# Head norm in a fused attention block: squares and last multiplication on GpSimd, inverse roots spread by DMA

## The chip, the cores and the metric

The kernel runs on one core of a Trainium2 chip. Times are microseconds of device time of one launch; less is better. The core's engines work side by side, each through its own queue in order, and hand work to each other by semaphores: TensorE (PE; PEld is its weight load), VectorE (DVE), ScalarE (ACT), GpSimd (POOL), and SyncE (SP), which here issues DMAs. Matrix products land in PSUM, eight banks of 128 x 512 numbers in float32; everything else is in SBUF.

## The reference

Input x has shape 8 x 512 x 512 (batch, token, feature), all in float32. Three residual steps follow each other: half of an expert layer on the normalised x (softmax router over 16 experts, the 256 best tokens of each expert, one expert matrix), a differential attention on the normalised x, and the same expert layer again. Attention, cut to what matters here:

```
q = rope(x @ Wq)   # 16 heads, each of two halves of D = 32
k = rope(x @ Wk)   # 4 key heads, each used by 4 heads
scores = softmax(causal(q . k / sqrt(D)))            # of both halves
diff = softmax(causal(scores[:, 0] - lam * scores[:, 1]))
att = diff @ v
att = att * rsqrt(mean(att * att over D) + 1e-8) * rms_w   # the head norm
att = att * (1 - LAM_INIT)
out = att.reshape(b, s, E) @ Wo
```

The head norm is what the change touches. It has one factor for each token and head: the inverse root of the mean of 32 squares.

## The kernel before, in words

The expert layers and a short preparation stand at the two ends; attention fills the time between some 220 and 1300 us. It is one loop written out by hand: `for k in range(K + 13)`, K = 176 passes, 22 for each of the 8 batches. A batch has two phases of 11 passes, one for each pair of key heads (`gp` 0 and 1); a pass is one "block", a part of a tile of 128 tokens. In pass k the engines work on several blocks at once, each at another stage: scores of block k + 1 (`scores`, L761), energies and first exponentials of block k (L777 on VectorE, L790 on ScalarE), `mask`, `factors` and `weigh` of block k - 1 on GpSimd (L828, L804, L814), then its `difference` on VectorE (L848), second exponentials of block k - 2 (`exps2`, L862), transposes of an earlier block (L882, copied by L898 and L900), and values (L913, copied by L926). `difference` reads what `weigh` writes.

Work that is not tied to a block is put into named slots of a pass by `at(offset, slot, fn)`, and `fill(k, slot)` emits it there. The slots in the order of a pass are "short" (after the transposes and values), "act mid" and "mid" (after the exponentials), "long" and "long 2" (large products; the next scores stand before, between or behind them, by the list PLACES), "dve" (before `difference`), "act" (the end of ScalarE's pass) and "pool" (the end of GpSimd's; its first instruction is made to wait for the pass's last difference). `rope_steps` projects q and k for the next phase (L635), multiplies by cosine and sine on VectorE (L654, L656), swaps neighbouring rows by two DMAs on SP's queue (L662) and adds on GpSimd (L665). `norm_steps` normalises the next batch's x (h, L574, turned at L582).

`finish_steps` is the head norm and the output projection of one tile of 128 tokens, 32 tiles in all. Its parts stand at offsets o0 to o4 of a phase. The four offsets of a tile in the first phase after its batch, or in the second phase of it, are in `plan`; the last two tiles of the last batch take theirs from LAST.

- `square` (o0, "act"): ScalarE squares the 128 x 512 attention values aT (L683). The values are not divided by z, the sum of the second softmax, so the term 1e-8 becomes 1e-8 z squared: two more squares of z, scaled by the root of 1e-8, for even and odd heads (L685, the tile u).
- `sums` (o1, "short"): TensorE sums the squares of each head with the matrix hsum (L694) into 4 of 32 rows of ss, and adds u by products with the matrix both (L700).
- `root` (o1, "act mid"): ScalarE takes the logarithm and the exponential of -0.5 of it, which is the inverse root r (L707, L708). Rows without a head get a constant idle, so that the logarithm has an argument.
- `turn` (o3, "short"): sixteen small TensorE products with a row of the identity copy each row of r to the 32 rows of its head (L715), into a PSUM bank.
- `norm` (o3, "dve"): VectorE multiplies aT by that (L723).
- `pe` (o4, "long" and "long 2") and `residual` (one pass later, "mid"): the output projection (L731) and the addition to x (L737).

PSUM banks 6 and 7 (MISC) go in turn to the values, the projections, ss, the spread factors and the output projection: each takes the bank that was taken two before, and waits for its reader.

Of the kernel before, what the change touches and what calls it, by code (L numbers as in the profile page):

```python
# [16 lines left out]
P = 128  # L17
# [5 lines left out]
R = H // KVH  # L23
Q = P // 2
NEXP = 16
TOPK = B * S // NEXP
# [15 lines left out]
def macaron_kernel(  # L42
# [46 lines left out]
    for base, mult in ((0, 1), (D - 1, -1)):  # L89
        nc.gpsimd.affine_select(  # L90
            out=hsum, in_=hsum, compare_op=ALU.is_ge, fill=0.0, base=base,
            pattern=[[-D * mult, 32]], channel_multiplier=mult,
        )

    idle = keep.tile([P, 1], F32, name="idle")
    nc.vector.tensor_reduce(
        idle, ident.rearrange("p (c k) -> p c k", c=4)[:, :, 4:], AX.XY, ALU.add
    )

# [55 lines left out]

    LAST = ((0, 1, 1, 2, 3), (3, 4, 4, 5, 6))

# [385 lines left out]
    def attention(f0, f1, home, first_end, projections_end, drain):  # L543
# [128 lines left out]
        def finish_steps(at, os, b, i, st):  # L672

            name = f"f{b}_{i}"
            t = {}

            def square():
                t["sq"] = home["sq"].tile([P, 4, P], F32, name=f"{name}_sq", tag="sq", bufs=2)

                t["u"] = tiny.tile([P, 2, 4, 4], F32, name=f"{name}_u", tag="u")  # L680
                z2 = st["z2"][:, i * H : (i + 1) * H]
                uh = t["u"].rearrange("p f c (q h) -> p (f c q) h", h=2)
                nc.scalar.activation(t["sq"], st["aT"][i], AF.Square)  # L683
                for h in range(2):
                    nc.scalar.activation(  # L685
                        uh[:, :, h], z2, AF.Square, scale=root_eps[:, h : h + 1]
                    )

            def sums():


                t["ss"] = misc(f"{name}_ss")
                for c in range(4):
                    nc.tensor.matmul(  # L694
                        t["ss"][32 * c : 32 * (c + 1), :P], hsum, t["sq"][:, c, :],
                        start=True, stop=False, tile_position=(0, 32 * c),
                    )
                for f in range(2):
                    for c in range(4):
                        nc.tensor.matmul(  # L700
                            t["ss"][32 * c : 32 * c + 4, f * Q : (f + 1) * Q], t["u"][:, f, c],
                            both, start=False, stop=(f == 1), tile_position=(0, 32 * c),
                        )

            def root():
                r = t["r"] = tiny.tile([P, P], F32, name=f"{name}_r", tag="r")
# [3 lines left out]
            def turn():  # L710

                t["f"] = misc(f"{name}_f")
                for c in range(4):
                    for q in range(4):
                        nc.tensor.matmul(  # L715
                            t["f"][q * D : (q + 1) * D, c * P : (c + 1) * P],
                            ident[:, 32 * c + q : 32 * c + q + 1].to_broadcast([P, D]), t["r"],
                            start=True, stop=True, tile_position=(0, q * D),
                        )

            def norm():
                t["an"] = home["sq"].tile([P, 4, P], F32, name=f"{name}_an", tag="sq", bufs=2)
# [15 lines left out]

            o0, o1, o2, o3, o4 = os
# [6 lines left out]
            at(o4, "long 2", lambda: pe(1))  # L746
            at(o4 + 1, "mid", residual)

# [237 lines left out]
        def plan(ph):  # L986
# [3 lines left out]
            if gp == 0:  # L990
# [77 lines left out]
        for k in range(K + 13):  # L1068
# [274 lines left out]
```

## Time and profile before

| what | value |
|---|---|
| median of 3 runs (lowest to highest) | 1422.42 us (1417.44 to 1423.59) |
| span of the profiled execution | 1420.2 us |
| TensorE's granted clock over the span | 0.969 |
| ScalarE: square of aT, L683 | 32 x 632 ns |
| ScalarE: squares of z, L685 | 64 x 302 ns |
| TensorE: spreading products, L715 | 35.0 us in 32 tiles |
| VectorE: last multiplication, L723 | 32 x 683 ns |
| GpSimd: rope addition of 128 x 512, L665 | 80 x 1296 ns |
| SP: swap by DMA, L662 | 160, 128 KB each, 2.0 us to landing |

The profile is of one execution; its own time is its span. A row of a group gives line, engine, operation, what is written and read, the count, then busy us and mean ns of one, then the engine's idle time just before and who ended it. A row of a time line gives start, length, then the same. The chain is the work that ended last, followed back from the end of the launch: what stands on it set the time.

### The profile page before, as it was taken

Reading aid. Unit: us, or ns where it says so; the run is one execution under the profiler, and the core shown is the slowest. Engines: PE = TensorE matmul, PEld = TensorE weight load, DVE = VectorE, ACT = ScalarE, POOL = GpSimd, SP = SyncE. Lnnn points to the kernel's source line nnn. Section 1 sums busy time; section 2 is a strip of 40 time slices with the busy share of each in tenths; the row PEclk is TensorE's granted clock in tenths of the full one; section 3 lists DMA queues with packets and bytes.
Section 4 is the critical chain, followed back from the end, with each engine's and each line's share of the span. In section 5 each row is a group of like instructions: output and inputs, shape, how many; then the busy total and the mean of one; then the engine's idle time right before and its main releaser. Section 6 shows DMA issues by size and latency. Waiting matters only on the chain.

```text
span 1420.2 us, 30675 instructions
## 1 busy us (share of the span) xinstructions
PE 1328.5 (94%) x9774; PEld 738.4 (52%) x9774; DVE 1154.9 (81%) x4405; ACT 1047.0 (74%) x3644; POOL 685.4 (48%) x1314
## 2 busy tenths in 40 slices
PE   6999899899999999999999999999999997998998
PEld 4544444455555555555555555555455555555443
DVE  6554769899989988998999899889989989654566
ACT  3411128999899898989898998989899989844110
POOL 5433626554555455454545555554545555443230
PEclk9999988999999999999999999999999997999999
DMA  9300011000000101000000001010000001000006
GB/s 344 91 1 0 0 38 38 9 31 24 16 24 17 39 1 38 9 31 9 32 24 16 28 13 39 2 38 16 24 13 27 28 13 40 1 5 1 1 1 236
DMA packets 27554, 48.19 MB, mean 34 GB/s; under 512 B 4720, under 2 KB 6016, under 8 KB 27392
## 3 DMA queue, kind: packets, MB, share of 16 engines
q1 hardware_dynamic: 25152, 42.03, 8.3%
q10 hardware_dynamic: 2208, 4.19, 0.8%
q8 instruction: 77, 1.26, 0.4%
q14 instruction: 85, 0.70, 0.2%
q0 software_dynamic: 32, 0.01, 0.0%
HBM read 16.86 MB, written 8.39 MB: 18 GB/s over the span
## 4 chain that ended last, share of the span: by engine, by line
PE 60%; ACT 13%; DVE 10%; issue 2%; POOL 0%; ACTq 0%; DVEq 0%
PE r_ps L635 18%; PE sc L761 8%; PE f_o L731 8%; ACT e L790 7%; PE tp L882 6%; PE yps L381 6%; PE av L913 4%; DVE e L777 4%; DVE t L848 3%; ACT t L862 2%; PE vps L610 2%; PE kps L403 2%; PE f_f L715 1%; ACT eT L900 1%; PE tp L325 1%
## 5 line engine op out<-in xcount | busy, mean ns | idle before, releaser
L790 ACT ACTIVATE e<-e,nb 128x192 f32<-128x192 f32 (+7 forms) x1024 | 535.5, 532 | 6.5 <-DVE nb L777 4.3
L777 DVE CUSTOM_DVE_ANT_0 e<-sc,mpos 128x192 f32<-128x192 f32 (+7 forms) x1024 | 400.8, 453 | 23.7 <-PE sc L761 16.5
L814 POOL TENSOR_SCALAR e<-e,z 128x512 f32<-128x512 f32 (+7 forms) x512 | 295.9, 590 | 16.7
L862 ACT ACTIVATE t<-t,nm 128x512 f32<-128x512 f32 (+7 forms) x512 | 270.0, 534 | 42.2 <-DVE nm L848 42.0
L761 PE MATMUL sc<-r,r 32*128 32x64 f32 (+7 forms) x2048 | 245.3, 456 | 10.8 <-DVE nb L777 4.9
L848 DVE CUSTOM_DVE_ANT_0 t<-e,z 128x512 f32<-128x512 f32 (+7 forms) x512 | 240.6, 518 | 5.1 <-POOL e L814 4.2
L635 PE MATMUL r_ps<-hT,wq_sb 128*128 128x512 f32 x512 | 235.6, 601 | 0.1
L381 PE MATMUL yps<-we,y 128*128 128x512 f32 x456 | 216.5, 612 | 1.0 <-ACT y L388 0.7
L882 PEld LDWEIGHTS tp<-ident,t 128*128 128x128 f32 x1280 | 146.5, 144 | 135.6 <-ACT eT L900 43.3
L882 PE MATMUL tp<-ident,t 128*128 128x128 f32 x1280 | 188.6, 283 | 28.1 <-ACT eT L900 26.6
L790 ACT ACTIVATION_READ_ACCUMULATOR e<-e,nb 128x1 f32 x1024 | 202.1, 197 | 0.0
L665 POOL TENSOR_TENSOR r<-r,r_sw 128x512 f32<-128x512 f32 x80 | 103.0, 1296 | 175.8 <-DVE z L799 84.2
L761 PEld LDWEIGHTS sc<-r,r 32*128 32x128 f32 x2048 | 117.4, 188 | 90.7 <-DVE nb L777 44.6
L391 POOL TENSOR_TENSOR y<-y,eb 128x512 f32<-128x512 f32 x57 | 73.1, 1283 | 164.4 <-ACT y L388 134.3
L635 PEld LDWEIGHTS r_ps<-hT,wq_sb 128*128 128x128 f32 x512 | 93.0, 190 | 113.9 <-issue 99.6
L388 ACT COPY y<-yps 128x512 f32<-128x512 f32 x57 | 33.4, 586 | 155.6 <-PE yps L381 155.6
L828 POOL TENSOR_SCALAR_AFFINE_SELECT e<-e 128x128 f32<-128x128 f32 x256 | 79.2, 316 | 99.4 <-ACT e L790 99.4
L898 DVE COPY eT<-tp 128x512 f32<-128x512 f32 (+1 forms) x176 | 112.0, 636 | 16.6 <-PE tp L882 16.6
L381 PEld LDWEIGHTS yps<-we,y 128*128 128x128 f32 x456 | 81.3, 192 | 78.4 <-issue 73.6
L731 PE MATMUL f_o<-wo_sb,f_an 128*128 128x512 f32 x256 | 118.6, 605 | 0.0
L804 POOL TENSOR_TENSOR z<-z,over 128x4 f32<-128x4 f32 (+1 forms) x192 | 38.0, 201 | 142.6 <-DVE z L799 142.5
L862 ACT ACTIVATION_READ_ACCUMULATOR t<-t,nm 128x1 f32 x512 | 100.4, 196 | 0.0
(123 smaller groups left out, 1668.6 us busy)
## 6 DMA issues: line engine op xcount, KB each, us to landing
r_sw<-r_by SPq DMA_DIRECT2D x160, 128.0 KB, 2.0
x<-in_x_dram SPq DMA_DIRECT2D x6, 1024.0 KB, 13.2
out_dram<-x SPq DMA_DIRECT2D x6, 512.0 KB, 3.2
out_dram<-x ACTq DMA_DIRECT2D x6, 512.0 KB, 3.2
x<-in_x_dram SPq DMA_DIRECT2D x8, 256.0 KB, 8.2
we<-in_expert_w_dram SPq DMA_DIRECT2D x2, 1024.0 KB, 7.7
wq_sb<-in_wq_dram SPq DMA_DIRECT2D x1, 2048.0 KB, 13.9
wo_sb<-in_wo_dram SPq DMA_DIRECT2D x8, 128.0 KB, 2.8
```

The source lines that it names most:

```text
L381: nc.tensor.matmul(held["yps"], buf[b][:, i, c * P : (c + 1) * P], held["we"][:, c, :], start=(c == 0), stop=(c == EC - 1),)
L635: nc.tensor.matmul(t["ps"], w[:, c, c0 : c0 + P], st["hT"][:, c, :], start=(c == 0), stop=(c == EC - 1),)
L665: return nc.gpsimd.tensor_add(t["out"], t["out"], t["sw"])
L731: nc.tensor.matmul(t["o"], t["an"][:, c, :], wo_sb[:, c // 2, c % 2, :], start=(c == 0), stop=(c == 3),)
L761: nc.tensor.matmul(u["sc"][j][:, part.cols], q[j * D : (j + 1) * D, q0 : q0 + P], kq["k"][j * D : (j + 1) * D, : part.n], start=True, stop ...
L777: nc.vector.tensor_tensor_reduce(out=u["e"][:, j, part.cols], in0=u["sc"][j][:, part.cols], in1=mpos[:, S - part.n :], scale=1.0, scalar=3 ...
L790: nc.scalar.activation(e, e, AF.Exp, bias=u["nb"][:, c : c + 1], scale=-1.0, accum_out=u["z"][:, 0, c : c + 1],)
L814: nc.gpsimd.tensor_scalar(e, e, u["z"][:, 1, c : c + 1], u["z"][:, 0, c - nr : c - nr + 1], ALU.mult, ALU.mult,)
L848: u["diff"] = nc.vector.tensor_tensor_reduce(out=u["t"][:, par, r * w : r * w + part.n], in0=u["e"][:, 2 * par, s], in1=u["e"][:, 2 * par ...
L862: nc.scalar.activation(t, t, AF.Exp, bias=u["nm"][:, par, r : r + 1], scale=-1.0, accum_out=z2[:, col : col + 1],)
L882: nc.tensor.transpose(u["tp"][par][:, o : o + P], u["t"][:, par, (r * (i + 1) + c) * P : (r * (i + 1) + c + 1) * P], ident,)
L898: nc.vector.tensor_copy(o, s)
```

## The change

Squares and last multiplication move to GpSimd for 30 tiles; the last two tiles of the last batch keep the old way, under the names `square_late`, `turn_late` and `norm_late`. The matrix hsum and the tile u are made eightfold (REP = 8), so that all 32 rows of a group of four heads hold a sum, each head in eight equal rows; u is written by GpSimd from z squared and a constant, two instructions of 128 x 128 a tile. The root no longer needs the constant idle. The sums move from the slot "short" to a new slot "sums" ahead of "long", the root from "act mid" to "act". The spreading products are replaced by four DMAs on SP's queue (`spread`), each reading 32 rows of r and writing every row to four rows, into the tile that held the squares; the last multiplication is done there in place. h no longer shares buffers with the squares.

```diff
@@ hsum, constants
-            pattern=[[-D * mult, 32]], channel_multiplier=mult,
+            pattern=[[-D * mult, 4], [0, REP]], channel_multiplier=mult,
...
+    eps_of = keep.tile([P, 2], F32, name="eps_of")
+    nc.vector.tensor_scalar(eps_of, parity, RMS_EPS, None, ALU.mult)
...
-    LAST = ((0, 1, 1, 2, 3), (3, 4, 4, 5, 6))
+    LAST = ((0, 1, 2, 3), (3, 4, 5, 6))
@@ finish_steps
+            def factor_tile():
+                t["u"] = tiny.tile([P, 2, 4, 4 * REP], F32, name=f"{name}_u", tag="u", bufs=1)
+                return t["u"].rearrange("p f c (q h w) -> p (f c q) h w", h=2, w=REP)
+
             def square():
                 t["sq"] = home["sq"].tile([P, 4, P], F32, name=f"{name}_sq", tag="sq", bufs=2)
-                nc.scalar.activation(t["sq"], st["aT"][i], AF.Square)
-                for h in range(2):
-                    nc.scalar.activation(
-                        uh[:, :, h], z2, AF.Square, scale=root_eps[:, h : h + 1]
-                    )
+                first = nc.gpsimd.tensor_tensor(t["sq"], st["aT"][i], st["aT"][i], ALU.mult)
+                z2 = st["z2"][:, i * H : (i + 1) * H]
+                zz = tiny.tile([P, H], F32, name=f"{name}_zz", tag="zz", bufs=1)
+                nc.gpsimd.tensor_tensor(zz, z2, z2, ALU.mult)
+                uh = factor_tile()
+                for h in range(2):
+                    nc.gpsimd.tensor_scalar(
+                        uh[:, :, h], zz.unsqueeze(2).to_broadcast([P, H, REP]),
+                        eps_of[:, h : h + 1], None, ALU.mult,
+                    )
+                return first
...
-                            t["ss"][32 * c : 32 * c + 4, f * Q : (f + 1) * Q], t["u"][:, f, c],
-                            both, start=False, stop=(f == 1), tile_position=(0, 32 * c),
+                            t["ss"][32 * c : 32 * (c + 1), f * Q : (f + 1) * Q],
+                            t["u"][:, f, c], both, start=False, stop=(f == 1), tile_position=(0, 32 * c),
...
-                nc.scalar.activation(r, t["ss"][:, :P], AF.Ln, bias=idle)
+                nc.scalar.activation(r, t["ss"][:, :P], AF.Ln)
...
+            def spread():
+                for c in range(4):
+                    nc.sync.dma_start(
+                        t["sq"][:, c, :],
+                        t["r"][32 * c : 32 * (c + 1), :].unsqueeze(1).to_broadcast([32, D // REP, P]),
+                    )
+
+            def norm():
+                t["an"] = t["sq"]
+                return nc.gpsimd.tensor_tensor(t["an"], t["an"], st["aT"][i], ALU.mult)
...
-            at(o0, "act", square)
-            at(o1, "short", sums)
-            at(o1, "act mid", root)
-            at(o3, "short", turn)
-            at(o3, "dve", norm)
-            at(o4, "long", lambda: pe(0))
+            if b == B - 1 and i > 1:
+                at(o0, "act", square_late)
+                at(o1, "short", sums)
+                at(o1, "act mid", root)
+                at(o2, "short", turn_late)
+                at(o2, "dve", norm_late)
+            else:
+                at(o0, "pool", square)
+                at(o1, "sums", sums)
+                at(o1, "act", root)
+                at(o1, "act", spread)
+                at(o2, "pool", norm)
+            at(o3, "long", lambda: pe(0))
...
@@ plan
-                    finish_steps(at, (0, 1, 2, 4, 5) if b < B else LAST[0], b - 1, 2, sts[b - 1])
-                    finish_steps(at, (3, 5, 5, 7, 8) if b < B else LAST[1], b - 1, 3, sts[b - 1])
+                    finish_steps(at, (0, 1, 4, 5) if b < B else LAST[0], b - 1, 2, sts[b - 1])
+                    finish_steps(at, (3, 4, 7, 8) if b < B else LAST[1], b - 1, 3, sts[b - 1])
...
-                finish_steps(at, (4, 5, 5, 7, 9), b, 0, sts[b])
-                finish_steps(at, (6, 7, 7, 9, 10), b, 1, sts[b])
+                finish_steps(at, (4, 5, 7, 9), b, 0, sts[b])
+                finish_steps(at, (6, 7, 9, 10), b, 1, sts[b])
@@ the pass
+            fill(k, "sums")
             fill(k, "long")
@@ first_end
-        home.update(aT=opened["out"], sq=opened["out"], h=(opened["out"], "sq"))
+        home.update(aT=opened["out"], sq=opened["out"], h=(opened["out"], "h"))
```

More of the change, by code (lines that the diff above doesn't have):

```diff
@@ L24 @@
 Q = P // 2
+REP = 8
 NEXP = 16
@@ L90, in macaron_kernel @@
         nc.gpsimd.affine_select(
-            out=hsum, in_=hsum, compare_op=ALU.is_ge, fill=0.0, base=base,
-            pattern=[[-D * mult, 32]], channel_multiplier=mult,
-        )
-    idle = keep.tile([P, 1], F32, name="idle")
-    nc.vector.tensor_reduce(
-        idle, ident.rearrange("p (c k) -> p c k", c=4)[:, :, 4:], AX.XY, ALU.add
-    )
+            out=hsum.rearrange("p (q w) -> p q w", w=REP), in_=hsum.rearrange("p (q w) -> p q w", w=REP),
+            compare_op=ALU.is_ge, fill=0.0, base=base,
+            pattern=[[-D * mult, 4], [0, REP]], channel_multiplier=mult,
+        )
     parity = keep.tile([P, 2], F32, name="parity")
@@ L675, in finish_steps, with square_late @@
             t = {}
+            def factor_tile():
+                t["u"] = tiny.tile([P, 2, 4, 4 * REP], F32, name=f"{name}_u", tag="u", bufs=1)
+                return t["u"].rearrange("p f c (q h w) -> p (f c q) h w", h=2, w=REP)
             def square():
                 t["sq"] = home["sq"].tile([P, 4, P], F32, name=f"{name}_sq", tag="sq", bufs=2)
-                t["u"] = tiny.tile([P, 2, 4, 4], F32, name=f"{name}_u", tag="u")
+                first = nc.gpsimd.tensor_tensor(t["sq"], st["aT"][i], st["aT"][i], ALU.mult)
                 z2 = st["z2"][:, i * H : (i + 1) * H]
-                uh = t["u"].rearrange("p f c (q h) -> p (f c q) h", h=2)
+                zz = tiny.tile([P, H], F32, name=f"{name}_zz", tag="zz", bufs=1)
[7 more added lines that the diff above has]
+                return first
+            def square_late():
+                t["sq"] = home["sq"].tile([P, 4, P], F32, name=f"{name}_sq", tag="sq", bufs=2)
+                z2 = st["z2"][:, i * H : (i + 1) * H]
+                uh = factor_tile()
                 nc.scalar.activation(t["sq"], st["aT"][i], AF.Square)
@@ L685, in square @@
                     nc.scalar.activation(
-                        uh[:, :, h], z2, AF.Square, scale=root_eps[:, h : h + 1]
+                        uh[:, :, h], z2.unsqueeze(2).to_broadcast([P, H, REP]), AF.Square,
+                        scale=root_eps[:, h : h + 1],
                     )
@@ L700, in sums, with turn_late @@
                         nc.tensor.matmul(
-                            t["ss"][32 * c : 32 * c + 4, f * Q : (f + 1) * Q], t["u"][:, f, c],
-                            both, start=False, stop=(f == 1), tile_position=(0, 32 * c),
+                            t["ss"][32 * c : 32 * (c + 1), f * Q : (f + 1) * Q],
+                            t["u"][:, f, c], both, start=False, stop=(f == 1), tile_position=(0, 32 * c),
                         )
             def root():
-                r = t["r"] = tiny.tile([P, P], F32, name=f"{name}_r", tag="r")
-                nc.scalar.activation(r, t["ss"][:, :P], AF.Ln, bias=idle)
+                r = t["r"] = tiny.tile([P, P], F32, name=f"{name}_r", tag="r", bufs=1)
+                nc.scalar.activation(r, t["ss"][:, :P], AF.Ln)
                 nc.scalar.activation(r, r, AF.Exp, scale=-0.5)
-            def turn():
+            def spread():
[7 more added lines that the diff above has]
+                return nc.gpsimd.tensor_tensor(t["an"], t["an"], st["aT"][i], ALU.mult)
+            def turn_late():
                 t["f"] = misc(f"{name}_f")
@@ L716, in turn, with norm_late @@
                             t["f"][q * D : (q + 1) * D, c * P : (c + 1) * P],
-                            ident[:, 32 * c + q : 32 * c + q + 1].to_broadcast([P, D]), t["r"],
+                            ident[:, 32 * c + REP * q : 32 * c + REP * q + 1].to_broadcast([P, D]), t["r"],
                             start=True, stop=True, tile_position=(0, q * D),
                         )
-            def norm():
+            def norm_late():
                 t["an"] = home["sq"].tile([P, 4, P], F32, name=f"{name}_an", tag="sq", bufs=2)
@@ L737, in residual @@
                 nc.vector.tensor_add(x_sb[b][:, i, :], x_sb[b][:, i, :], t["o"])
-            o0, o1, o2, o3, o4 = os
-            at(o0, "act", square)
-            at(o1, "short", sums)
-            at(o1, "act mid", root)
-            at(o3, "short", turn)
-            at(o3, "dve", norm)
-            at(o4, "long", lambda: pe(0))
-            at(o4, "long 2", lambda: pe(1))
-            at(o4 + 1, "mid", residual)
+            o0, o1, o2, o3 = os
+            if b == B - 1 and i > 1:
[11 more added lines that the diff above has]
+            at(o3, "long", lambda: pe(0))
+            at(o3, "long 2", lambda: pe(1))
+            at(o3 + 1, "mid", residual)
         def scores(u):
```

## The prediction

> **What bounds the kernel now.** I read the page first (engine shares, the chain), then the table of stretches for one whole batch of attention, the chain in order of time over that batch, and last the time lines of GpSimd (POOL) and VectorE (DVE) in the passes where the change puts work. Page, parts 1 and 4:
>
> ```profile
> PE 1328.5 (94%) x9774; PEld 738.4 (52%) x9774; DVE 1154.9 (81%) x4405; ACT 1047.0 (74%) x3644; POOL 685.4 (48%) x1314
> ...
> PE 60%; ACT 13%; DVE 10%; issue 2%; POOL 0%; ACTq 0%; DVEq 0%
> ```
>
> One stretch of 135 us inside attention (start:end, length, then busy us of PE, PEld, DVE, ACT, POOL; the batch period is about 130 us):
>
> ```profile
> 740.00:875.00 135.00, 128.65 (x1127) 72.80 (x1126) 122.81 (x498) 125.22 (x456) 72.37 (x152) 0.99 0.06 23
> ```
>
> PE 95%, ACT 93%, DVE 91%: three engines are close to full at once, POOL is at 54%. So the kernel is not bound by one engine but by the order in which the three hand work to each other. The chain shows who leads where (start, length, what):
>
> ```profile
> 752.54 0.61 DVE r_by L656
> ...
> 753.19 1.08 PE f_f L715 x32
> ...
> 758.81 3.63 PE f_o L731 x8
> ...
> 828.67 0.53 ACT f_sq L683
> 829.21 0.40 ACT f_u L685 x2
> ...
> 839.29 1.01 PE f_f L715 x32
> ...
> 841.92 3.63 PE f_o L731 x8
> ```
>
> Number the loop's passes 0 to 21 in a batch. Passes 0 to 3 and 11 to 15 are TensorE's (projections). Pass 4 hangs on f_f, then VectorE. Passes 16 to 19 are ScalarE's, with the squares on the chain. From pass 20's output projection, at 841.92, TensorE leads again without a gap until pass 3 of the next batch: what is lost by then is not won back there.
>
> **What the change removes.** For 30 of the 32 head-norm tiles: on ScalarE the square (L683, 632 ns) and two squares of z (L685, 302 ns each), 1.24 us; on TensorE 16 spreading products, L715 35.0 us / 32 = 1.09 us; on VectorE one multiplication, L723 683 ns. In all 37, 33 and 20 us of busy time. The part that lies on the chain between 218 and 1310 us is smaller: summed by line, f_f 19.2 us (2.0 of it in the two tiles that stay), f_sq and f_u 7.6, f_an 1.4, together 26 us. That is the most that removal alone can give.
>
> **What it adds.** The eight small products get 32 columns of weights instead of 4: loads of 88 ns become 110 ns (L700 against L694), under matmuls; nothing. SP gets 120 DMAs: L662 issues take about 0.5 us each and land after 2.0 us, so four take some 4 us from the root to the landing, while the last multiplication stands 2 to 3 passes (over 9 us) later. On SP's queue the spreads stand ahead of rope's swaps only in pass 1: issued by about 737.4 (root 735.3 plus four issues), against a swap that VectorE has ready at 739.5. Nothing gained or lost, with 2 us to spare; if one came late POOL would wait with everything behind it. The inverse root now stands at the end of ScalarE's pass, behind sums that follow the scores: in pass 1 it ends near 735.3 instead of 734.2 and pushes ScalarE by 0.6 us, which TensorE's lead in passes 2 and 3 hides. h gets buffers of its own, the constants change: nothing on the path (TensorE waits 0.7 us for h in a batch at most, the end unmoved).
>
> What matters is POOL. Its "pool" slot opens when VectorE's differences (L848) of the pass are done, and the next pass's weighing (L814), which the next differences need, stands behind that slot on the same queue. Rows:
>
> ```profile
> L665 POOL TENSOR_TENSOR r<-r,r_sw 128x512 f32<-128x512 f32 x80 | 103.0, 1296 | 175.8 <-DVE z L799 84.2 <-DVE nm L848 70.8 <-DVE r L654 14.2
> L814 POOL TENSOR_SCALAR e<-e,z 128x128 f32<-128x128 f32 x64 | 28.0, 445 | 0.0
> L228 POOL TENSOR_SCALAR wo_sb<-wo_sb,rms_sb 128x512 f32<-128x512 f32 x4 | 6.2, 1570 | 0.1
> L224 POOL TENSOR_SCALAR rms_sb<-rms_sb 128x1 f32<-128x1 f32 x1 | 0.2, 245 | 0.0
> ```
>
> A square or a last multiplication is 1.28 us (L665, L391). z squared: 0.2 us (L1158). The two widened factors are a form that before does not have at this size: one operation, 128x128. L228 and L224, the same one-operation form, give 245 ns plus 2.6 ns an element, so 0.58 us each; low end 0.445, the two-operation form of that size; high end 0.9, since the writes go in runs of eight. I take 0.58, the same form. A square slot is then 1.28 + 0.2 + 1.16 = 2.64 us (2.4 to 3.3).
>
> The Trainium skill ("GPSIMD Engine Reference", section 4.1) says of elementwise work to use VectorE, GpSimd being about twice as slow with two inputs and near line rate with one. The rows bear out the first half (1296 against 683 ns). By the second half, as an estimate, a factor would be near 0.4 us and the loss below some 7 us instead of 12; the 1570 ns row speaks against it here.
>
> Passes 15 to 20 of one batch. Slots 15 and 17 already hold a rope addition:
>
> ```profile
> 828.97 1.31 POOL L665 TENSOR_TENSOR r<-r,r_sw 128x512 f32<-128x512 f32 x1 [2.15 <-DVE z L799]
> 830.23 0.29 POOL L828 TENSOR_SCALAR_AFFINE_SELECT e<-e 128x128 f32<-128x128 f32 x1
> 830.49 0.20 POOL L804 TENSOR_TENSOR z<-z,over 128x4 f32<-128x4 f32 x1
> 830.79 1.31 POOL L814 TENSOR_SCALAR e<-e,z 128x384 f32<-128x384 f32 x2
> ...
> 832.27 0.61 DVE L848 CUSTOM_DVE_ANT_0 t<-e,z 128x384 f32<-128x384 f32 x1
> ```
>
> - Pass 16: slot 15 opens at 819.1; the first half of the weighing ended at 821.6 and now ends at 824.3, the differences started at 823.84. VectorE loses 0.65 us by their end.
> - Pass 18: slot 17 opens 0.65 late, at 829.6; addition 1.26, square 2.64, mask, z and half the weighing 1.25: 834.8. The differences started at 832.27; they end at 836.05 instead of 833.38, 2.7 us late. VectorE's saved 0.6 us is eaten by this wait.
> - Pass 19 keeps it. ScalarE, 0.9 us lighter, now waits for VectorE. Pass 20: energies to 843.1, the last scores 0.45 later, the output projection at 843.6 instead of 841.85: 1.75 us late. TensorE's saved f_f falls into its own wait here, and so does its new wait in pass 18, where the sums find POOL's factors ready at 833.6 only: its next scores need VectorE's energies at 837 and later.
>
> Passes 3 to 5: slot 3 holds an addition and a square. Without f_f and f_an the differences of pass 4 could start at 754.1 instead of 754.94, but POOL is ready at 754.85 only: 0 gained (0.85 at most, if POOL were free). Slot 4 holds an addition and a multiplication: the differences of pass 5 start at 759.9 instead of 758.57, hidden behind the output projection, which runs to 762.4.
>
> Sum: seven batches with projections in their second half, 7 x 1.75 = 12.3 us lost; the first halves, 0; the last batch, where ScalarE's squares (1.0) and two f_f (2.1) were on the chain and passes last 8 us, about 2 gained. Together +10 us on the profiled execution's 1420.2 us. That is 2 us under the median of the runs, 1422.4; I forecast 1431 us. With 0.445 us a factor a pass-20 delay of 1.1 gives +6; with 0.9 us it is 3.0 and passes 3 to 5 lose 0.6: +23.
>
> **Rivals.** (a) Faster. POOL's slots are covered because the three engines shift together: ScalarE, lighter by 1.24 us in passes 15 and 17, would have to lead VectorE's next wait. Then up to the 26 us of the chain comes off: 1396, or 1410 with half of it. For it: POOL idles 46% and waits 84.2 us for z at L665; against it: its slot and weighing in pass 18 are 5.2 us where 3.4 lay between differences. It decides in favour of faster when the square slot stays under about 1.6 us. (b) Neither: factors near 0.3 us make the square slot 2.1; passes 3 to 5 then gain 0.55 and pass 20 loses 0.65: 0.1 x 7, 1421. (c) Much slower: POOL's two-input operations meet VectorE's. The row for it is L535, two inputs from SBUF, 737 ns at the least and 1829 at the most when L391 runs beside it, while L777, with one from PSUM, keeps 488 ns for 320 columns beside L665. The differences have two SBUF inputs. The gate keeps them apart, so I count this only if slots run long: 0.7 us (between nothing and the 1.09 us that L535 lost at most) on each of four passes, 7 x 2.8, on top of the forecast: 1451. The Trainium skill, "SBUF — State Buffer", section "Who interferes with whom", calls this an exclusive lock that makes the second wait for the whole first; then one collision would cost 1.28 us, not 0.7.
>
> **How the numbers follow.** Forecast (1425 to 1445) 0.48, (a) 0.25, (b) 0.19, (c) 0.08. The two runs 1417.4 and 1423.6 of before lie 0.4% apart, so about 0.5% (7 us) is what a measurement can tell. Of the forecast's chance 0.05 falls within that bound and of (b)'s 0.01 outside: faster 0.25, within 0.5% 0.23, slower 0.52. Range: down to 1403, which leaves out the stronger half of (a), up to 1450, most of (c) out. The likeliest case alone: 1425 to 1445.
>
> **What would show it.** f_f and f_sq down to two tiles' worth; POOL near 60% busy; the widened factors at 0.45 to 0.9 us; "DVE t waits for POOL e", 4.2 us in before, at 15 us or more, in passes 16, 18 and 5; the batch period at 131 to 132 us. The prediction is wrong if that wait stays under 8 us, if the period falls below 129, or if TensorE or POOL waits on the spread's DMA.

## The result and the profile after

The kernel after takes 1459.63 us (median of 4 runs, 1458.46 to 1461.11) against 1422.08 for the kernel before measured beside it: 1.0269 times as long, 95% interval 1.0249 to 1.0289. Forecast were 1431 us and a range from 1403 to 1450. The direction was right, the size was not.

The page of the kernel after, parts 1 and 4, answers to the first lines shown of before (engine shares, then the chain by engine):

```profile
PE 1372.2 (94%) x8814; PEld 756.7 (52%) x8814; DVE 1138.7 (78%) x4375; ACT 1024.7 (70%) x3554; POOL 798.3 (55%) x1464
...
PE 48%; DVE 17%; ACT 9%; POOL 9%; issue 3%; POOLq 0%; DVEq 0%; ACTq 0%
```

VectorE and ScalarE have less to do, as meant; GpSimd has 113 us more and now holds 9% of the chain, where it held none. The line that should stop a reader is the first figure: TensorE executes 960 matmuls fewer (8814, before 9774) and is busy 44 us longer (1372.2, before 1328.5). Its work has shrunk and its time has grown, so it works more slowly. The granted clock over the span says so: 0.929, before 0.969.

One batch of each (start:end, length, busy us of PE, PEld, DVE, ACT, POOL, granted clock, DMA share, GB/s), before first:

```profile
856.24:985.88 129.64, 123.38 (x1076) 69.97 (x1075) 117.62 (x478) 119.85 (x434) 68.27 (x146) 0.99 0.06 22
```

```profile
888.10:1024.63 136.53, 130.95 (x947) 73.47 (x947) 115.62 (x474) 117.04 (x422) 83.67 (x166) 0.91 0.09 28
```

A batch of the steady ones in the middle grows by 6.9 us, and the clock in it falls from 0.99 to 0.91. Over the launch: the first seven batches 41.0 us more (5.9 each on average), the last 3.5 less, what lies before the first differences 1.4 more, which is the 38.9 us between the two spans (1459.1 and 1420.2).

The chain of the kernel after through passes 18 to 21 of one batch (start, length, what). Before, its counterpart was ScalarE's squares, then f_f and f_o:

```profile
992.42 1.28 POOL r L664
993.70 1.00 POOL f_sq L682
994.70 0.17 POOL f_zz L685
...
994.98 1.18 POOL f_u L688 x2
996.15 0.25 POOL e L862
996.40 0.17 POOL z L838
...
997.33 1.05 POOL e L848
...
998.40 0.62 DVE t L882
...
1004.43 3.70 PE sc L795 x8
1008.13 5.82 PE f_o L758 x8
...
1016.75 3.63 PE f_o L758 x8
```

Two things are to be seen. Down to 998.40 the chain is the one that the prediction drew: rope's addition, the square slot (993.70 to 996.15), mask, z, half the weighing, and the differences start at once. Then comes what it did not draw: an output projection, the same eight matmul records each time, takes 5.82 us at 1008.13 and 3.63 at 1016.75, and 3.63 in the kernel before.

The clock in steps of 3.41 us around that place, TensorE alone (start:end, length, busy us, granted clock, DMA share, GB/s), kernel after:

```profile
985.19:988.60 3.41, 3.41 (x58) 1.00 0.13 43
988.60:992.02 3.42, 3.05 (x17) 1.00 0.44 119
992.02:995.43 3.41, 3.29 (x11) 0.50 0.00 1
995.43:998.84 3.41, 3.41 (x34) 0.50 0.00 0
998.84:1002.26 3.42, 3.42 (x34) 0.50 0.32 76
1002.26:1005.67 3.41, 2.84 (x16) 1.00 0.00 0
1005.67:1009.08 3.41, 3.41 (x7) 0.50 0.02 5
1009.08:1012.50 3.42, 3.42 (x6) 0.50 0.00 0
1012.50:1015.91 3.41, 3.41 (x48) 1.00 0.00 0
```

The clock is granted in whole steps of 3.41 us, either full or half. Half steps follow stretches where TensorE waits for VectorE, and the two around 1009 lie under the output projection that TensorE leads with. In the seven batches with projections before has 44 us of half steps in all, after 160.

What makes a step half was counted. For each matmul record, take rows x columns x moving columns, spread over its duration, and set the sum in a step against what back-to-back records of 128 x 128 x 512 at 454 ns (f_o's eight in 3.63 us) would do. This is called the step's work here. Over the 18 profiles of this case there are 5408 steps between 225 and 1250 us. In 417 of them the work is less than 0.39; 406 of these are followed at once by a half step. There are 416 half steps in all, and of 4964 steps with 0.40 or more only 2 are followed by one. With the bound at 0.39, 21 steps go against the rule. Counting only how many columns moved, the best bound misses some 290, and counting the busy time itself some 380. The step at 988.60 shows why the busy time misleads: 3.05 of 3.42 us busy, but its work is 0.36, since scores use 32 of 128 rows and matmuls that wait count as busy.

The Trainium skill, "TensorE: Matmul & The Clock Gate", Part 1, has the free-running window of 3413 ns and the half rate after an idle window; the steps above agree with the length and the rate. It speaks of idle windows; the five steps above after which the clock is halved hold 2.84 to 3.41 us of busy time, and what they lack is work (0.27 to 0.39). Here the measurement decides.

The waits behind this, kernel after (engine line, waited for: us, times, longest):

```profile
ACT t L896 <- DVE nm L882: 55.7, 75, 2.1
DVE t L882 <- POOL e L848: 43.3, 61, 2.2
DVE x L764 <- PE f_o L758: 35.6, 22, 5.4
```

```profile
PE sc L795 <- DVE nb L811: 15.7, 33, 1.8
```

Before these were 42.0, 4.2, 13.0 and 4.9 us: GpSimd holds up VectorE, VectorE holds up ScalarE and TensorE, and the residual waits for the slow projection.

### The profile page after: what moved, and what is told of

Its sections match the earlier page's. It is cut to its first block, busy times and chain, and to the rows that moved or that the text cites. A ratio compares the mean times of both kernels' runs of the same rounds, so it can differ in the third digit from the quotient of the medians.

```text
span 1459.1 us, 29153 instructions
## 1 busy us (share of the span) xinstructions
PE 1372.2 (94%) x8814; PEld 756.7 (52%) x8814; DVE 1138.7 (78%) x4375; ACT 1024.7 (70%) x3554; POOL 798.3 (55%) x1464
## 4 chain that ended last, share of the span: by engine, by line
PE 48%; DVE 17%; ACT 9%; POOL 9%; issue 3%; POOLq 0%; DVEq 0%; ACTq 0%
PE r_ps L634 11%; PE f_o L758 9%; PE sc L795 8%; DVE e L811 6%; DVE t L882 5%; ACT e L824 5%; PE yps L380 5%; PE tp L916 4%; PE av L947 4%; POOL e L848 2%; ACT t L896 2%; POOL r L664 2%; PE vps L609 2%; PE kps L402 2%; POOL f_u L688 2%
## 5 line engine op out<-in xcount | busy, mean ns | idle before, releaser
L848 POOL TENSOR_SCALAR e<-e,z 128x512 f32<-128x512 f32 (+7 forms) x512 | 305.3, 609 | 16.8
L795 PE MATMUL sc<-r,r 32*128 32x64 f32 (+7 forms) x2048 | 285.7, 485 | 21.4 <-DVE nb L811 15.7
L882 DVE CUSTOM_DVE_ANT_0 t<-e,z 128x512 f32<-128x512 f32 (+7 forms) x512 | 242.6, 516 | 43.4 <-POOL e L848 43.3
L916 PEld LDWEIGHTS tp<-ident,t 128*128 128x128 f32 x1280 | 151.6, 147 | 108.1 <-issue 38.8
L916 PE MATMUL tp<-ident,t 128*128 128x128 f32 x1280 | 191.1, 290 | 12.7 <-ACT eT L934 11.3
L795 PEld LDWEIGHTS sc<-r,r 32*128 32x128 f32 x2048 | 143.8, 197 | 110.3 <-DVE nb L811 63.2
L824 ACT ACTIVATION_READ_ACCUMULATOR e<-e,nb 128x1 f32 x1024 | 198.1, 194 | 0.0
L758 PE MATMUL f_o<-wo_sb,f_sq 128*128 128x512 f32 x240 | 132.9, 704 | 0.0
L934 ACT COPY eT<-tp 128x512 f32<-128x512 f32 (+1 forms) x176 | 94.3, 536 | 32.5 <-PE tp L916 32.1
L947 PE MATMUL av<-eT,v 128*32 128x128 f32 (+1 forms) x2176 | 100.2, 318 | 0.0
```

Of the source, the lines that this page charges most:

```text
L758: nc.tensor.matmul(t["o"], t["an"][:, c, :], wo_sb[:, c // 2, c % 2, :], start=(c == 0), stop=(c == 3),)
L795: nc.tensor.matmul(u["sc"][j][:, part.cols], q[j * D : (j + 1) * D, q0 : q0 + P], kq["k"][j * D : (j + 1) * D, : part.n], start=True, stop ...
L824: nc.scalar.activation(e, e, AF.Exp, bias=u["nb"][:, c : c + 1], scale=-1.0, accum_out=u["z"][:, 0, c : c + 1],)
L848: nc.gpsimd.tensor_scalar(e, e, u["z"][:, 1, c : c + 1], u["z"][:, 0, c - nr : c - nr + 1], ALU.mult, ALU.mult,)
L882: u["diff"] = nc.vector.tensor_tensor_reduce(out=u["t"][:, par, r * w : r * w + part.n], in0=u["e"][:, 2 * par, s], in1=u["e"][:, 2 * par ...
L916: nc.tensor.transpose(u["tp"][par][:, o : o + P], u["t"][:, par, (r * (i + 1) + c) * P : (r * (i + 1) + c + 1) * P], ident,)
```

## The experiments

Two figures in the expectations below are mistaken and are put right here. First, a "dead product" of 128 x 128 x 512 leaves two matmul records, at 454 ns each back to back, so it costs 0.9 us and counts 0.27 of a step, not 0.45 and 0.133; the sixteen spreading products of a tile are the same 0.27, in 1.09 us. Second, the "10.4 us" between a low step and its half step is an offset between the clock records' zero and the first instruction; the half step follows directly. "Halved us" are half steps summed over a batch.

The times are medians, each with its ratio to before and the interval of it. The clock is that of the profiled execution, from which batches and steps are read; in a_sq_act this was one of the two fastest (1418.2 us; eight others took 1422 to 1426 us at 0.952 to 0.954), in b_sq_pool the slowest (1472.0).

| run | what | us | ratio | clock |
|---|---|---|---|---|
| after | | 1459.63 | 1.0269 [1.0249, 1.0289] | 0.929 |
| a_sq_act | after, squares and u on ScalarE | 1425.37 | 1.0012 [0.9996, 1.0028] | 0.959 |
| a_dead_f | after, spreading products as dead work | 1443.89 | 1.0157 [1.0133, 1.0181] | 0.956 |
| b_sq_pool | before, squares and u on GpSimd | 1462.14 | 1.0264 [1.0236, 1.0291] | 0.939 |
| b_no_f | before without spreading products | 1438.65 | 1.0110 [1.0092, 1.0127] | 0.949 |
| a_bank | after, banks stepped on, no instruction added | 1453.82 | 1.0229 [1.0211, 1.0247] | 0.932 |
| a_dense | after, one dead dense product a tile | 1442.33 | 1.0149 [1.0134, 1.0164] | 0.957 |
| a_fill | after, 14 dead products a batch | 1439.43 | 1.0121 [1.0106, 1.0137] | 0.985 |
| sq_act_fill | a_sq_act, the same 14 | 1418.73 | 0.9982 [0.9971, 0.9992] | 0.984 |
| a_late_fill | after, square behind the weighing, 14 | 1429.28 | 1.0047 [1.0032, 1.0062] | 0.978 |
| a_u_act_fill | after, u alone on ScalarE, 14 | 1416.47 | 0.9959 [0.9944, 0.9973] | 0.977 |
| sq_act_fill2 | a_sq_act, 8 dead products | 1427.01 | 1.0026 [1.0014, 1.0038] | 0.965 |
| b_fill | before, 3 dead products | 1412.31 | 0.9928 [0.9914, 0.9943] | 0.983 |
| b_one | before, 1 dead product | 1419.32 | 0.9974 [0.9965, 0.9984] | 0.972 |
| b_half | before, half a dead product | 1419.18 | 0.9972 [0.9960, 0.9984] | 0.973 |
| b_elsewhere | before, 3 dead products where no step is low | 1436.05 | 1.0107 [1.0082, 1.0131] | 0.968 |
| b_sq_pool_fill | b_sq_pool, 14 dead products | 1432.87 | 1.0076 [1.0061, 1.0091] | 0.984 |

### Which part of the change: GpSimd's slot, or TensorE's missing work

Squares and factors back on ScalarE, all else as in the kernel after:

```diff
-                at(o0, "pool", square)
+                at(o0, "act", square_late)
```

> The kernel after, with the squares (and the factors u) back on ScalarE; the last multiplication stays on GpSimd, the spread stays a DMA, the spreading products stay gone. Theory 1 (GpSimd's square slot ahead of the weighing holds VectorE up, and the gaps that this leaves in TensorE's work halve its clock): 'DVE t waits for POOL e' falls from 43 us to under 15, the granted clock returns from 0.929 to 0.96 or more, time 1405 to 1425 us. Theory 2 (TensorE's clock falls because the spreading products are gone from it): the products are still gone, so the clock stays under 0.945 and the time above 1440. Theory 3 (GpSimd's operations slow VectorE and the transfers by contention, about in proportion to what GpSimd does): half of the added GpSimd work is gone, about half of the 37 us comes back, 1438 to 1445.

Measured 1425.4 us: the loss is gone, and nothing more. The wait of the differences for GpSimd falls to 15.7 us. All three figures of Theory 1 are missed by a hair (15, 0.96, 1425). Theory 2 as it stood falls (the products are gone and the clock is 0.959, 1425 us), and so does Theory 3, which gave only half of the loss back; but the full 0.969 does not return.

Spreading products put back as dead work:

```diff
                 at(o1, "act", spread)
+                at(o2, "short", turn_late)
```

> The kernel after, with the sixteen spreading products of each tile put back on TensorE at their old place, into a bank that nobody reads (dead work; the output is the same). Theory 1 (the GpSimd slot is the cause, the halved clock its consequence): no help, clock 0.92 to 0.94, 1455 to 1475 us, because the products fall into TensorE's wait. Theory 2 (the missing products lower the clock): clock 0.955 or more, 1425 to 1442 us.

Measured 1443.9 us, clock 0.956: sixteen products a tile that nobody reads make the kernel 16 us faster, though the wait for GpSimd stays (41.8 us). So Theory 1 is not the whole either, and the time lies between what the two theories gave. Halved us a batch go from 23.9 down to between 6.8 and 10.2 in the steady batches.

The kernel before without the spreading products:

```diff
-                t["an"] = home["sq"].tile([P, 4, P], F32, name=f"{name}_an", tag="sq", bufs=2)
-                nc.vector.tensor_tensor(
-                    t["an"], st["aT"][i], t["f"].rearrange("p (c q) -> p c q", c=4), ALU.mult
-                )
+                t["an"] = t["sq"]
+                nc.vector.tensor_tensor(t["an"], st["aT"][i], t["sq"], ALU.mult)
...
-            at(o3, "short", turn)
```

This kernel leaves out the spreading of the inverse roots, so what it computes is not the head norm.

> The kernel before without the sixteen spreading products: VectorE's last multiplication reads the squares in SBUF in place of the spread inverse root (this leaves out the spreading of the inverse root over the rows of its head). No work is added anywhere. Theory 1: nothing new stalls, the clock stays at 0.96 or more and a part of the 17 us that the products had on the chain comes off: 1405 to 1422 us. Theory 2: clock 0.945 or less, 1430 us or more.

Measured 1438.7 us: 35 us of TensorE's work taken away, none added elsewhere, and the kernel is 16 us slower. Two of its batches show how (columns as in the batches above):

```profile
603.17:733.94 130.77, 123.97 (x948) 69.22 (x948) 117.66 (x478) 119.63 (x434) 69.59 (x146) 0.99 0.06 21
...
869.04:1005.71 136.67, 130.95 (x948) 72.20 (x947) 117.85 (x478) 119.89 (x434) 69.63 (x146) 0.91 0.06 21
```

The same 948 matmuls take 124.0 us in one batch and 131.0 in the other. Without the products, a step in pass 5 falls to some 0.25 in most batches, in the shorter one shown too, and steps in passes 8, 9, 18 and 19 to between 0.31 and 0.41, close to the bound; whether one falls below it depends on how the steps cut the pass. (VectorE's multiplication, now with both operands in SBUF, takes 776 ns in place of 683, 3 us in all.)

The squares alone on GpSimd, products kept:

```diff
...
-            at(o0, "act", square)
-            at(o1, "short", sums)
-            at(o1, "act mid", root)
+            if b == B - 1 and i > 1:
+                at(o0, "act", square)
+                at(o1, "short", sums)
+                at(o1, "act mid", root)
+            else:
+                at(o0, "pool", square_pool)
+                at(o1, "sums", sums)
+                at(o1, "act", root)
...
```

> The kernel before, with the squares and the factors u alone moved to GpSimd (u of 128 x 64, so a slot of some 1.04 + 0.2 + 2 x 0.4 = 2.0 us), the sums and the root moved to the later places as in the kernel after; spreading products on TensorE and the last multiplication on VectorE stay. Theory 1: the slot is most of the stall: 'DVE t waits for POOL e' 20 us or more, clock 0.935 to 0.955, 1435 to 1455 us. Theory 2: the products are there, clock 0.96 or more, at most 1430 us.

Measured 1462.1 us, more than either theory gave: this part alone costs as much as the whole. The wait of the differences is 14.6 us only, under the 20 expected, but 17.1 us a batch are halved. That left open whether the moved sums and root did it; the last experiment of this chapter answers in part.

From these four a combined theory, called 1+2' in the expectations: a stall (from the slot) and missing work both lower what TensorE does in a step, and below 0.39 the next step runs at half.

### Is it the work, and what is left when the clock is mended

> The kernel after, where each tile, at the place of the old spreading products, only steps the turn of PSUM banks 6 and 7 on by one, as the products' bank did; no instruction is added. It tells whether the 15 us that the dead products won back were the products' work or the order of the banks. Theory 4 (the order of the banks decides who waits for which reader): 1440 to 1448 us. Theory 2' (counted over six traces: TensorE's clock is halved for a step of 3.4 us about 10.4 us after a step in which it did less than 0.39 of the multiplications that back-to-back 128 x 128 x 512 products at 454 ns would do; 21 of 1803 steps go against this): no work is added, so 1455 to 1463 us and clock 0.925 to 0.935.

The edit only steps the turn of the two banks (`turns[MISC] += 1` at o2, "short"). Measured 1453.8 us, between the two theories: 6 of the 16 us. The order of the banks isn't the main cause. In the profiled execution four half steps fewer lie in the first seven batches (147 us halved, after 160), and these are 4 us shorter together; why the bank order saves half steps wasn't settled.

```diff
+            def dense():
+                nc.tensor.matmul(misc(f"{name}_d"), ident, cosk, start=True, stop=True)
...
+                at(o2, "short", dense)
```

> The kernel after with one dead 128 x 128 x 512 product a tile (0.45 us) at the place of the old sixteen spreading products (1.09 us): the same number of multiplications in under half the time. Theory 2' (multiplications per step count): about the same clock as with the sixteen dead products (0.956), 1437 to 1446 us. If time in which TensorE is busy counted, less than half of the 15 us would come back: 1450 to 1458 us.

Measured 1442.3 us and 0.957, as with the sixteen. Since the product really costs 0.9 us against 1.09, this run doesn't tell work from busy time, as it was meant to; the count over all profiles does.

Dead products ahead of the transposes, in passes with low steps:

```diff
+        FILL = {4: 1, 5: 2, 8: 1, 9: 1, 11: 2, 17: 2, 18: 2, 19: 2, 20: 1}
...
+            for _ in range(extra):
+                nc.tensor.matmul(u["tp"][0], ident, cosk, start=True, stop=True)
...
-                turn_pe(u2)
+                turn_pe(u2, FILL.get(k % 22, 0))
```

> The kernel after with dead 128 x 128 x 512 products ahead of the transposes in the passes where a step fell under 0.39: one in passes 4, 8, 9, 20, two in passes 5, 11, 17, 18, 19 of every batch (14 of 0.45 us, 6.3 us of TensorE a batch, mostly in waits). Theory 1+2' (the slot's direct loss is what the prediction said, some 10 us, and the rest is the halved clock): clock 0.965 or more, 1425 to 1440 us. If the stall itself is the whole loss and the clock only goes with it: clock up, time 1450 us or more, since the dead products come on top.

Here `FILL` gives the number of dead products by the pass of a batch. The same list on the kernel of a_sq_act:

> The kernel after with the squares on ScalarE (1425 us, clock 0.959), with the same dead products. Theory 1+2': without the slot and without the halved clock a part of the 26 us that the removed work had on the chain comes off: clock 0.97 or more, 1400 to 1415 us, faster than both kernels. If the removed work was covered anyway: 1418 to 1428 us.

Measured 1439.4 and 1418.7 us. One batch of each, a_fill first:

```profile
866.90:998.43 131.53, 129.46 (x976) 71.47 (x975) 115.59 (x474) 117.07 (x422) 83.78 (x166) 1.00 0.09 29
```

```profile
850.90:979.64 128.74, 127.08 (x975) 70.39 (x975) 115.38 (x475) 120.07 (x434) 73.75 (x150) 1.00 0.09 30
```

Some 12.7 us of TensorE's work were added to each batch of the kernel after, and it is 5.0 us shorter, at full clock, while the differences' wait for GpSimd stays at 41.4 us. Between the two, with the same dead products and no halved clock, lie 2.8 us a batch: this is the price of squares and factors in GpSimd's slot against squares and factors on ScalarE. Of the 5.0 us, 1.4 are not new: the kernel before has a half step in each steady batch too, and the run b_fill below is 1.4 us a batch shorter without it. So of the 6.9 us a batch, 3.6 go with added half steps, 2.8 with the slot, and 0.5 are left, about what the dead products of passes 8 and 9 cost (pass 9 grows by 0.6). The split isn't exact, since dead products stand in part on the chain. The second run missed its 1400 to 1415 and came out at the end of its other range (1418 to 1428), that the removed work was covered anyway; the last batch pays 6 us for dead products (150.6 against 144.5).

Time between the ends of the last differences of one pass and the next, us, median of five batches:

| pass | before | after | a_fill | sq_act_fill |
|---|---|---|---|---|
| 4 | 6.97 | 6.47 | 6.46 | 5.87 |
| 5 | 4.25 | 5.47 | 5.49 | 5.49 |
| 6 | 5.35 | 5.83 | 4.48 | 4.52 |
| 13 | 8.99 | 8.96 | 7.65 | 7.65 |
| 16 | 5.95 | 6.71 | 6.72 | 5.95 |
| 18 | 4.58 | 6.70 | 6.71 | 4.15 |
| 20 | 5.17 | 4.22 | 4.22 | 4.43 |
| 21 | 5.65 | 9.41 | 6.25 | 6.26 |
| all 22 | 129.6 | 136.6 | 131.5 | 128.7 |

After and a_fill differ by more than 0.15 us in passes 6, 13 and 21 alone (and by 0.6 the other way in pass 9): there the half steps lie under work that TensorE leads with.

### The slot: its place and its length

The square behind the next pass's weighing, sums and root a pass later:

```diff
-                at(o0, "pool", square)
-                at(o1, "sums", sums)
-                at(o1, "act", root)
-                at(o1, "act", spread)
+                at(o0 + 1, "pool 2", square)
+                at(o1 + 1, "short", sums)
+                at(o1 + 1, "act mid", root)
+                at(o1 + 1, "act mid", spread)
...
                 weigh(u1)
+            fill(k, "pool 2")
```

> The kernel after with the dead products of a_fill (in the first seven batches only), and with the square and the factors placed behind the next pass's weighing on GpSimd's queue, not held until the differences are done; the sums and the root one pass later. GpSimd does the same work. Theory 1 (the order on GpSimd's queue makes the direct loss): 'DVE t waits for POOL e' from 41 to under 20 us, the batch period from 131.5 to 128.5 to 129.5 us, 1408 to 1420 us. Theory 3 (GpSimd's work slows VectorE by contention, and more so where it now runs beside the differences): the period stays at 131 us or more, the differences' mean of 516 ns grows, 1430 us or more.

Measured 1429.3 us, between the two theories: the wait falls to 22.6 us, the period is 130.8 where no step is halved and 132.3 where one is. The groups of the differences and of the square in this run:

```profile
L882 DVE CUSTOM_DVE_ANT_0 t<-e,z 128x512 f32<-128x512 f32 (+7 forms) x512 | 249.0, 531 | 22.8 <-POOL e L848 22.6
...
L682 POOL TENSOR_TENSOR f_sq<-aT 128x512 f32<-128x512 f32 x30 | 33.3, 1110 | 0.0
```

Differences of 531 ns instead of 516 and a square of 1110 instead of 1039: the two engines do disturb each other when they run side by side, by 6 us of VectorE over the launch (249.0, after 242.6). The means hide how. Only 8 of the 30 squares meet a difference, seven of them in pass 18: there a difference of 384 columns that starts 0.37 us into the square takes 1.38 us in place of 0.62 and ends 0.41 us after the square, and the square itself takes 1.34 in place of 1.04. In the kernel after, where the gate keeps them apart, the differences have 516 ns and before 518, so Theory 3 has no part in the loss. What holds passes 3 and 19 up in this run (0.6 and 1.2 us more than in a_fill) wasn't followed further.

Only the factors u back on ScalarE (`at(o0, "act", factors_act)`), the square stays in the slot:

> The kernel after with the same dead products (first seven batches), the square on GpSimd and only the factors u on ScalarE: a square slot of 1.04 us in place of 2.45. The prediction put the point from which a slot costs something at some 1.6 us. Theory 1: nearly all of the direct loss goes, period 128.7 to 129.7 us, 1408 to 1422 us. If any square slot costs in proportion to its length: some 130 us, 1422 to 1428 us.

Measured 1416.5 us, period 129.4: a slot of 1.04 us costs 0.7 us a batch where one of 2.45 costs 2.8. That is less than in proportion to the length (1.2 would be), as the prediction's point of some 1.6 us below which a slot is covered would have it, though not quite nothing; with two lengths the point itself isn't shown. This version, with dead products, is faster than the kernel before without any by 0.4%, and slower than the kernel before with three a batch (next section).

### The halved clock in the kernel before

The kernel before with the same means, three products a batch, in the first seven batches:

```diff
+        FILL = {11: 2, 18: 1}
```

> The kernel before with three dead products a batch in the first seven batches (two in pass 11, one in pass 18, where its steps are under or at 0.39). Theory 2': its halved steps, 3.4 us a batch, go, clock 0.975 or more, and the period falls from 129.6 by up to 1.7 us: 1409 to 1420 us. If the halved step falls where TensorE waits anyway: 1420 to 1424.

Measured 1412.3 us, the fastest of all. Its batch:

```profile
849.63:977.82 128.19, 122.78 (x1082) 70.05 (x1081) 117.52 (x478) 119.30 (x434) 68.12 (x146) 1.00 0.06 22
```

Six matmul records more, 0.6 us less busy, and 1.45 us shorter: the one half step of each steady batch is gone, and pass 13 takes 7.66 instead of 8.99.

The kernel of a_sq_act with `FILL = {4: 1, 7: 1, 11: 2, 17: 1, 18: 2, 19: 1}`, in the first seven batches:

> The kernel after with the squares on ScalarE and fewer dead products, in the first seven batches only (one in passes 4, 7, 17, 19, two in passes 11 and 18: 8 in place of 14 a batch). In the run with 14 the last batch took 150.6 us against 144.5 without any. Theory 2': period 128.5 to 129 us, last batch 144.5: 1408 to 1415 us, faster than both kernels.

Missed: 1427.0 us. With fewer dead products steps in passes 19 and 20 stay at 0.28 to 0.38 and the half step after them lies under the output projection (pass 21: 8.57 us).

The kernel before with `FILL = {11: 1}`, and with half the columns of that product:

> The kernel before with one dead 128 x 128 x 512 product in pass 11 of the first seven batches, and nothing else. The step there did 0.28 to 0.29 of back-to-back products in the profile of before; one product is 0.133, which makes 0.42, above the counted 0.39. Theory 2': the halved step of each batch goes, clock 0.975 or more, nearly all of the 10 us that three products won: 1411 to 1416 us.

> The same with half the product (256 columns): 0.28 + 0.067 = 0.35, under the counted 0.39. Theory 2' with its bound between 0.35 and 0.42: the halved steps stay, clock 0.965 to 0.972, 1419 to 1425 us. If what matters is not a bound but the work as such: half of the gain, 1415 to 1419 us.

Measured 1419.3 and 1419.2 us. The first missed, the second lies on the line between its two ranges, and the pair doesn't give the bound as meant. The product fell into the step before the low one, which rose from some 0.45 to some 0.7 and to between 0.53 and 0.59, and the low one stayed at 0.24 to 0.34 with its half step behind it. The 3 us gained are mostly one batch in which the steps cut the pass otherwise.

The kernel before with `FILL = {1: 2, 14: 1}`:

> The kernel before with as many dead products as in the run with three, but in passes 1 (two) and 14 (one), where the steps do 0.8 or more and TensorE leads. Theory 2': no halved step goes, and the products cost their 0.45 us each where TensorE leads: clock 0.965 to 0.972, 1423 to 1433 us. If dead products help for another reason (the weights or the bank), 1412 to 1418 us.

Measured 1436.1 us, above the 1433 named, where a product was taken at 0.45 us and not 0.9: the half steps stay, and the three products cost 2.3 us a batch. Dead work as such doesn't help; it must stand in a low step.

The kernel of b_sq_pool with the list of a_fill, in the first seven batches:

> The kernel before with the squares and factors alone on GpSimd (1462 us, clock 0.939, which neither theory had foreseen), with the 14 dead products a batch, in the first seven batches. Theory 1+2': its loss is the slot's (pass 18, some 1.6 us a batch) and the rest the halved clock in passes 6, 12 and 21: clock 0.975 or more, period 130 to 132 us, 1420 to 1436 us. If the later places of the sums and the root hold the kernel up by themselves: 1445 us or more.

Measured 1432.9 us, period 131.5 in place of 136.5, no half step in the steady batches. So the larger part of the loss of b_sq_pool, 5.0 of 6.9 us a batch, went with the halved clock as well. Against the kernel before at full clock (b_fill, 128.2) 3.3 us a batch are left; how they divide between the slot, the moved sums and root, and the dead products isn't shown.

## Why the prediction was wrong, point by point

- **The slot's price: right.** The rows of the kernel after:

```profile
L688 POOL TENSOR_SCALAR f_u<-f_zz,eps_of 128x128 f32<-128x128 f32 x60 | 35.4, 599 | 3.1
L682 POOL TENSOR_TENSOR f_sq<-aT 128x512 f32<-128x512 f32 x30 | 31.2, 1039 | 41.4 <-DVE nm L882 38.2 <-DVE z L833 3.2
L685 POOL TENSOR_TENSOR f_zz<-z 128x16 f32<-128x16 f32 x30 | 6.4, 213 | 0.0
```

  A factor is 0.60 us (taken: 0.58), the square 1.04 (taken: 1.28, the price of rope's addition, which reads two tiles and writes in place), together 2.45 against 2.64. The estimate of 0.4 us for a factor that the prediction worked out from the Trainium skill ("GPSIMD Engine Reference", section 4.1) is not borne out.
- **Where it bites in the second half of a batch: right, nearly to the tenth.** Counted from pass 16 on in the table of passes, the kernel after is 0.76 us late by pass 16 (forecast 0.65), 2.9 by pass 18 (2.7), 1.9 by pass 20 (1.75). The wait is 43.3 us where 15 or more were named. The last batch gains 3.5 us (forecast 2).
- **The first half: forecast 0, measured 1.2 us lost.** Pass 5 is later by the 1.2 us that the prediction saw (5.47, before 4.25), but pass 6, which was to hide it, grows as well (5.83, before 5.35). With the dead products pass 6 takes 4.48, so the forecast holds at full clock only.
- **What failed** is the step "TensorE's saved f_f falls into its own wait here, and so does its new wait in pass 18", and with it the sum 7 x 1.75. It took TensorE's idle time as free. That wait, without f_f in it, takes TensorE's steps below 0.39 of full work; the next ones run at half clock, and they lie under the output projection of pass 20, from which, as the prediction itself says, nothing is won back. Pass 21 grows by 3.76 us, 3.15 of which the dead products take away, and pass 6 by 0.48; none of this had a term in the sum. With the dead products in place the kernel after has the period that was forecast, 131.5 for 131 to 132, and 1439 us. That agreement is in part luck: the same products also take away the half step that the kernel before has under pass 13 (1.3 us), and against the kernel before at full clock (128.2) the change costs 3.3 us a batch, not 1.75.
- **The removed work:** of the 26 us on the chain, the 18.6 of f_f and f_an gave nothing that could be seen: squares on ScalarE, the rest of the change and full clock come to 128.7 us a batch (sq_act_fill, with 14 dead products), while the kernel before at full clock comes to 128.2 (b_fill, with 3). The forecast took the removal for covered up to pass 20, and so it was. What the squares' 7.6 us are worth no run shows by itself.
- **Spread, queue, root, h:** no wait on the spread's DMA shows; nothing, as taken.
- **Rivals.** (c) came nearest in time, 1451, for a reason that the runs exclude: in the kernel after the differences have 516 ns. Its price was well taken, though: where a difference does meet the square, in a_late_fill, it loses 0.76 us (taken: 0.7). The point given for (a), a slot under some 1.6 us, is not settled: with a slot of 1.04 us and dead products the time is 1416.5 us, under the kernel before (1422.5) but over the kernel before at full clock (1412.3). Of the prediction's own signs only the period clearly missed (136.5 us for 131 to 132), and none of those that it named for being wrong came up. It had no line on the clock, though the table of before gives 0.969 and not 1.

## What to carry to other kernels

Before TensorE's work is taken away, or a wait is put before it, look at the granted clock in short steps and at how much TensorE does in the thinnest of them: in this kernel a step of 3.4 us with less than 0.39 of dense work made the next one run at half speed, and idle time that looked free cost more than the wait itself. A busy time that grew while the number of matmuls fell was the sign. Where the thin steps can't be filled with real work, a few dense products that nobody reads, put exactly there, paid here (1422 to 1412 us); in passes that TensorE leads they cost (1436 us).

## What the hardware showed that was not expected

- Work, not time: a step in which TensorE is busy 3.05 of 3.42 us, mostly with scores of 32 rows, is followed by a half step (work 0.36).
- The half steps hold each other up: of the 416 half steps none does more than 0.57, so with a short wait the next is low too, and 176 of them are followed by another. Between 992 and 1012 us of the kernel after five of six steps are half.
- Batches settle on whole numbers of steps: 129.6 us before is 38 x 3.413, 136.55 after and 136.5 in b_sq_pool are 40 x 3.413, each for three or more batches in a row. That this is a lock between the half steps and the loop is only argued.
- On GpSimd a product of 128 x 512 takes 1.04 us when both inputs are the same tile (L682) and 1.28 with two different ones (L735, 1279 ns). All the dearer ones here also write over one of their inputs, so which of the two makes the price isn't shown.
